# Turned context rows: written to memory once, loaded in cross attention

## The chip, the cores and the metric

The kernel runs on one core of one Trainium2 chip. The metric is the device time of one execution in microseconds. All data is fp32. One core has the engines TensorE (PE; its weight loads are shown apart as PEld), VectorE (DVE), ScalarE (ACT), GpSimd (POOL) and SyncE (SP, which only issues transfers here), and 16 DMA engines that serve the queues of all of them.

## What is computed

A two-layer Perceiver block: 16 batches of 64 latents x of width 256, and a context of 1601 rows of width 256 per batch.

```python
# layer 0
K = ctx @ Wk.T + bk ; V = ctx @ Wv.T + bv          # all 16 x 1601 rows
# each latent, head (16) and sample (5) reads two neighbouring rows of K and V at an
# offset that the query decides, weighs them, and attends over its 5 samples
x = x + sampled_attention(layer_norm(x), K, V)
x = x + self_attention(layer_norm(x))
x = x + moe_top2_of_8(layer_norm(x))
# layer 1: cross attention with 16 heads of 64
txt, img = ctx[:, :77], ctx[:, 77:]                # 77 and 1524 rows
q = heads(layer_norm(x) @ Wq)
out = softmax(q @ heads(txt @ Wk).T / 8) @ heads(txt @ Wv) \
    + softmax(q @ heads(img @ Wk_ip).T / 8) @ heads(img @ Wv_ip)
x = x + out @ Wo + bo
x = x + state_space(layer_norm(x))
x = x + moe_top4_of_32(layer_norm(x)) + shared_expert
```

The context thus enters twice: in layer 0 through the projection to K and V of every row, and in layer 1 through the image rows.

## The kernel before

P = 128 is the number of partitions, D = 256 the width, KC = 2 the number of 128-blocks in it, B = 16 the batches, M = 1601 the context rows.

**Order.** The instructions of TensorE, VectorE and ScalarE run in the order in which the program issues them (a manual schedule, from L1515 on). A scheduler places those of SP and GpSimd; a queue is served in its order, so a transfer on SP that waits holds up those behind it. A tile is taken from a pool by a tag with so many buffers (`bufs`); a new tile waits for the last user of the buffer it takes.

**Keys and values** (`keys_values`, L368 to L410). The rows of a batch go in spans (L236): three of 512 rows (128 partitions of r = RP = 4 neighbouring rows each) and a last one of 65 rows (r = 1). For each span

- `cx_load` (L239) loads the rows into `cx` on SP's queue, two spans ahead, two buffers;
- TensorE turns them in blocks of 128x128 (`transposes`, its matmul is L152; input to the matmul `ident`), ScalarE copies the turned blocks to `cxt` (L397, two buffers);
- one span later (`held`) `project` multiplies `cxt` with the weights `wkv` (L87, `st<-wkv,cxt`, 512 columns), ScalarE copies the result to `kv` (L381, two buffers), and one transfer on ScalarE's queue writes `kv` to the table of the batch in device memory (L384, `tab<-kv`): 16 heads x 512 bytes for each partition.

The main loop (L1529) takes one such step after the other and puts filler work between them: the sampling positions (`samples`), the text keys and values (`texts`, which writes `ktd`, L523), the first middle blocks (`middle`), and at given due times the gathers of the sampled rows from the tables by GpSimd (`g<-tab`, L428) and the sampled attention on VectorE.

**Cross attention** (class `Cross`, L896). For a batch, `loads` (L904) fetches the image rows as they are, `cn` (128 partitions of 11 rows, and 116 of one more; two buffers; a column of ones is added for the sum of the exponentials). `turn` (L926) transposes them once more, 24 blocks of 128x128 (L152, `mm<-ident,cn`), and VectorE and ScalarE copy the result to `cT` (one buffer). So the same image rows are turned by TensorE twice in the kernel, in keys and values and here. A `step` (L1059) then works on one pair of heads of the 8 in a batch: scores from the turned rows (`st<-qf,cT`, three groups of 512 columns), their maximum on VectorE (L1079), subtraction and exponential to `pt` (L1119, L1120, and L1122, L1123 for the last 116 rows), and in the next step the product of `pt` with `cn` (L1048). `qf` is the query folded with the key weights (`fold`, L1004). The last step of each batch calls the turn of the next one, between the output `out` (L1089) and the first product:

```python
if hp == NHP - 1:
    self.turn(b + 1)
if old:
    po = bank()[:, : D + 1]
    self.product(n - 1, 0, po)
```

The turn of batch 0 stands in `begin` (L1164), before the first step. Filler work of other parts (`side`, `mid`, `late`) is called from within the steps.

The order of the image rows is free: softmax and product sum over all of them, so any order will do as long as the scores and `cn` have the same.

Of the kernel before, what the change touches and what calls it, by code (L numbers as in the profile page):

```python
# [11 lines left out]
AF = mybir.ActivationFunctionType  # L12
ALU = mybir.AluOpType
# [4 lines left out]
P = 128  # L18
B, S, D = 16, 64, 256
M = 1601  # L20
KC = D // P
# [13 lines left out]
H1, HD1, INNER, TEXT = 16, 64, 1024, 77  # L35
IMG = M - TEXT
NHP = H1 // 2
CM = IMG // P
CR = IMG - CM * P
NCH = CM + 1  # L40
NB = NCH // 4


NST, NCONV = 16, 4
# [20 lines left out]
def perceiver_kernel(ctx: ExitStack, tc: tile.TileContext, a: dict, out: bass.AP):  # L65
    nc = tc.nc

    def mk(pool, shape, tag, dtype=F32, bufs=None):
        return pool.tile(list(shape), dtype, tag=tag, name=tag, bufs=bufs)
# [9 lines left out]
    def copy(i, o, x):  # L79
        if i % 2:  # L80
            nc.scalar.copy(o, x)  # L81
        else:
            nc.vector.tensor_copy(o, x)

    def mm(o, pairs):
        for i, (l, r) in enumerate(pairs):
            nc.tensor.matmul(o, lhsT=l, rhs=r, start=i == 0, stop=i == len(pairs) - 1)  # L87
# [59 lines left out]
    def transposes(blocks, ncol=P):  # L147

        rows = blocks[0].shape[0]
        t = bank().rearrange("p (i n) -> p i n", n=P)  # L150
        for i, b in enumerate(blocks):
            nc.tensor.transpose(t[:ncol, i, :rows], b, ident[:rows, :rows])  # L152
        return t

    def load(pool, tag, src, shape, bufs=None):
        t = mk(pool, shape, tag, bufs=bufs)
        nc.sync.dma_start(out=t, in_=src)
        return t
# [74 lines left out]
    sp = tpp  # L233


    spans = [(b, m0, RP if M - m0 >= RP * P else 1) for b in range(B) for m0 in range(0, M, RP * P)]  # L236
    cxs = {}

    def cx_load(i):  # L239
        if i < len(spans):  # L240
            b, m0, r = spans[i]
            w = min(P, M - m0)
            cx = cxs[i] = mk(kvp, [P, RP, D], "cx", bufs=2)
            nc.sync.dma_start(
                out=cx[:w, :r, :], in_=a["ctx"][b, m0 : m0 + w * r, :].rearrange("(p r) d -> p r d", r=r)
            )
# [121 lines left out]
    def keys_values():  # L368

        held = kv = None  # L370

        def project(i, cxt, q):
            nonlocal kv
            b, m0, r = spans[i]
            w = min(P, M - m0)
            if q == 0:
                kv = mk(kvp, [P, H0, RP, 2 * HD0], "kv", bufs=2)
            for c in range(2 * q, min(2 * q + 2, r)):
                pk = big()
                mm(pk[:w], [(cxt[:, c, k, :w], wkv[:, k, :]) for k in range(KC)])  # L380
                nc.scalar.copy(kv[:w, :, c, :], pk[:w].rearrange("p (h e) -> p h e", h=H0))  # L381
            if 2 * q + 2 >= r:
                tab = tables[b // 2].rearrange("n e -> (n e)").rearrange("(b h m e) -> b h m e", b=2, h=H0, e=2 * HD0)
                nc.scalar.dma_start(  # L384
                    out=tab[b % 2, :, m0 : m0 + w * r, :].rearrange("h (p r) e -> p h (r e)", r=r),
                    in_=kv[:w, :, :r, :].rearrange("p h r e -> p h (r e)"),
                )

        for i, (b, m0, r) in enumerate(spans):
            w = min(P, M - m0)  # L390
            cx = cxs.pop(i)
            cxt = mk(kvp, [P, RP, KC, P], "cxt")
            steps = (r + 1) // 2
            for q in range(steps):
                m = min(2, r - 2 * q)
                tp = transposes([cx[:w, 2 * q + t, k * P : (k + 1) * P] for t in range(m) for k in range(KC)])
                nc.scalar.copy(  # L397
                    cxt[:, 2 * q : 2 * q + m, :, :w].rearrange("p r k n -> p (r k) n"), tp[:, : KC * m, :w]
                )
                if q + 1 == steps:  # L400
                    cx_load(i + 2)
                if held:
                    for part in range((held[2] + 1) // 2):
                        if min(part, steps - 1) == q:
                            project(held[0], held[1], part)
                yield
            held = (i, cxt, r)
        for q in range((held[2] + 1) // 2):
            project(held[0], held[1], q)
        yield  # L410
# [485 lines left out]
    class Cross:  # L896
# [7 lines left out]
        def loads(self, b):  # L904
            if b >= B:
                return

            cn = self.cn[b] = mk(self.xc, [P, NCH, D + 1], "cn", bufs=2)
            nc.gpsimd.memset(cn[:, :, D:], 1.0)
            nc.sync.dma_start(  # L910
                out=cn[:, :CM, :D], in_=a["ctx"][b, TEXT : TEXT + CM * P, :].rearrange("(p c) d -> p c d", c=CM)
            )
            nc.sync.dma_start(out=cn[:CR, CM, :D], in_=a["ctx"][b, TEXT + CM * P :, :])

        def text_loads(self, b):
            if b >= B:
# [9 lines left out]
        def turn(self, b):  # L926

            if b >= B:
                return
            cn = self.cn[b]  # L930
            ct = self.ctx[b] = mk(self.xc, [P, KC, NCH * P], "cT", bufs=1)
            i = 0
            for k in range(KC):
                d = slice(k * P, (k + 1) * P)
                for c in range(0, CM, 4):
                    n = min(4, CM - c)
                    blocks = [cn[:, c + i_, d] for i_ in range(n)]
                    tp = transposes(blocks)
                    copy(i % 3, ct[:, k, c * P : (c + n) * P].rearrange("p (i n) -> p i n", n=P), tp[:, :n, :])
                    i += 1  # L940
                tp = transposes([cn[:CR, CM, d]])
                nc.scalar.copy(ct[:, k, CM * P : IMG], tp[:, 0, :CR])

                nc.scalar.copy(ct[:, k, IMG:], ct[:, k, : NCH * P - IMG])

        def queries(self, t, part):

# [94 lines left out]
        def product(self, n, part, po):  # L1042

            b = n // NHP
            pt, cn = pts[n % 2], self.cn[b]
            for c in range(part * 4, part * 4 + 4):
                w = P if c < CM else CR
                nc.tensor.matmul(po, lhsT=pt[:w, c, :], rhs=cn[:w, c, :], start=c == 0, stop=c == NCH - 1)  # L1048

        def turn_out(self, n):  # L1050
# [8 lines left out]
        def step(self, side=None, mid=None, more=None, late=None):  # L1059
# [11 lines left out]
            for i in range(NB):  # L1071
                if live:
                    s = big().rearrange("p (c n) -> p c n", n=P)
                    for c in range(4):
                        j = (i * 4 + c) * P
                        mm(s[:, c, :], [(ct[:, k, j : j + P], qf[:, k, :]) for k in range(KC)])
                    st.append(s)
                if live:
                    nc.vector.tensor_reduce(mp_[:, i, :], s.rearrange("p c n -> p n c"), AX.X, ALU.max)  # L1079
                    if i:  # L1080
                        nc.vector.tensor_tensor(mp_[:, 0, :], mp_[:, 0, :], mp_[:, i, :], ALU.max)
                if i == 1 and n - 2 < last:
                    self.turn_out(n - 2)
                if i == 1 and more is not None:
                    next(more, None)
                if i == 0:
                    tick(4.3)
# [25 lines left out]
            if live:  # L1113
                pt = pts[n % 2]
                for i in range(NB):
                    c0 = i * 4
                    m = 4 if i + 1 < NB else 3
                    o = pt[:, c0 : c0 + m, :]
                    nc.vector.tensor_tensor(o, st[i][:, :m, :], mc.to_broadcast([P, m, P]), ALU.subtract)  # L1119
                    nc.scalar.activation(o, o, AF.Exp)  # L1120
                o = pt[:CR, CM, :]
                nc.vector.tensor_tensor(o, st[-1][:CR, 3, :], mc[:CR, 0, :], ALU.subtract)  # L1122
                nc.scalar.activation(o, o, AF.Exp)  # L1123
            if late is not None:
                next(late, None)
            if old:
# [29 lines left out]
        def begin(self, xp):  # L1156
            self.xp = xp
            self.text_loads(0)
            self.weights(0, 0)
            yield  # L1160
            for part in range(3):
                self.queries(0, part)
                yield
            self.turn(0)  # L1164
            self.loads(1)
            yield
            self.text(0, 0)
            yield
            self.text(0, 1)
            self.text_turn(0, 0)  # L1170
            yield
            self.text_turn(0, 1)
            self.fold(0)
            yield
# [340 lines left out]
    with tc.manual_schedule(engines={ET.PE, ET.DVE, ET.Activation}):  # L1515
        for z in qbds:
            nc.gpsimd.memset(z, 0.0)
        for z in pts:
            nc.gpsimd.memset(z[:, CM, :], 0.0)
        nc.sync.dma_start(out=rsc, in_=a["rscale"].rearrange("(k p) -> p k", p=P))  # L1520
        nc.sync.dma_start(out=rws, in_=a["router0"].rearrange(kp, p=P))
        xbo = biases(const, "xbo", ("xbo",), a["bias_a"])["xbo"]
# [35 lines left out]
        xc = sx.enter_context(tc.tile_pool(name="xc", bufs=1))  # L1558
        cr = Cross(xc)
        cr.loads(0)  # L1560

        mids = middle(1, lp, single=True)
        while attended() < 12:
# [157 lines left out]
```

## Time and profile before

| | us |
|---|---|
| median of 3 runs | 3315.74 |
| lowest and highest | 3312.72, 3335.57 |
| the profiled execution | 3330.78 |
| its span | 3329.1 |
| PE busy in the span | 2961.7 (89%) |
| DVE busy | 1620.5 (49%) |
| ACT busy | 1024.3 (31%) |
| POOL busy | 809.0 (24%) |

The span is the time from the first to the last instruction of the profiled execution. Its mean granted TensorE clock was 0.944 of full speed. Keys and values end at about 715 us, cross attention runs from about 960 to 3040 us. A group of the profile is named by engine, line, operation and output<-input (partitions x elements); "mean ns of one" follows its busy time, and then the idle time of the engine before it, with what ended most of it. A matmul line gives first the tile of the stationary operand. The releasers are inferred from semaphores. In the table by stages each engine has its busy time and the number of its instructions; then come the granted clock, the mean busy share of the 16 DMA engines, and their rate.

### The profile page before, as it was taken

The numbers are of one execution on the slowest core, as the hardware profiler recorded it, in microseconds if no ns is written. First come the engines' busy times: TensorE is split into PE (matmuls) and PEld (weight loads), VectorE is DVE, ScalarE is ACT, GpSimd is POOL, SyncE is SP. The second block draws the span as 40 slices with busy tenths as digits, with TensorE's granted clock in tenths as the row PEclk, the third lists the DMA queues.
The fourth block names the chain that finished last, engine by engine and source line by source line (L and its number), as shares of the span: only waits on it lengthen the run. The fifth ranks groups of instructions, "written<-read, shape, count | busy, mean of one in ns | idle before, by whom it ended". The sixth has DMA issues, their size and how long they took to land.

```text
span 3329.1 us, 46406 instructions
## 1 busy us (share of the span) xinstructions
PE 2961.7 (89%) x17710; PEld 2420.5 (73%) x17710; DVE 1620.5 (49%) x4130; ACT 1024.3 (31%) x2366; POOL 809.0 (24%) x919
## 2 busy tenths in 40 slices
PE   8789887894878788889989999999999999998879
PEld 4444444562667777778878999999989999996666
DVE  3321113223334444445654335776577568665746
ACT  3233333322122221122333343333343344222421
POOL 0444434445334333432000001010001002000721
PEclk9889998996988899989999999999999999999999
DMA  7387755562321111111213542111112122003884
GB/s 230 100 152 160 219 162 155 169 183 55 116 65 24 43 42 55 26 54 41 73 38 116 165 128 72 56 60 50 49 61 55 50 70 65 30 1 119 254 235 121
DMA packets 338710, 326.19 MB, mean 98 GB/s; under 512 B 59301, under 2 KB 289097, under 8 KB 337977
## 3 DMA queue, kind: packets, MB, share of 16 engines
q1 hardware_dynamic: 186473, 226.04, 22.6%
q10 hardware_dynamic: 126640, 62.79, 6.8%
q0 software_dynamic: 25376, 34.39, 4.9%
q8 instruction: 141, 2.31, 0.3%
q14 instruction: 80, 0.66, 0.1%
HBM read 248.90 MB, written 74.22 MB: 97 GB/s over the span
## 4 chain that ended last, share of the span: by engine, by line
PE 74%; DVE 10%; another core or an unknown queue 5%; issue 5%; ACT 3%; DMA 2%; POOL 0%; SPq 0%; ACTq 0%; DVEq 0%; POOLq 0%
PE st L87 30%; PE mm L1048 19%; PE mm L87 16%; PE mm L152 4%; PE mm L1004 2%; DMA wg<-in_guT 1%; PE mm L1034 1%; PE mm L973 1%; DVE hs L1287 1%; DVE mp L1079 1%; PE mm L1098 1%; ACT pt L1120 1%; DMA w<-in_gate 0%; DVE pt L1119 0%
## 5 line engine op out<-in xcount | busy, mean ns | idle before, releaser
L428 POOL DMA_INDIRECT g<-tab,ig x640 | 610.3, 954 | 876.8 <-DVE ig L426 662.2
L87 PE MATMUL st<-qf,cT 128*128 128x128 f32 x6144 | 762.5, 282 | 57.0 <-ACT qf L1007 32.6
L87 PEld LDWEIGHTS st<-qf,cT 128*128 128x128 f32 x6144 | 740.3, 198 | 65.1 <-ACT qf L1007 36.4
L1048 PE MATMUL mm<-cn,pt 128*128 128x257 f32 (+1 forms) x3072 | 757.9, 391 | 0.2 <-ACT cT L81 0.2
L1048 PEld LDWEIGHTS mm<-cn,pt 128*128 128x128 f32 (+1 forms) x3072 | 565.7, 194 | 87.2 <-issue 2.0
L87 PE MATMUL st<-wkv,cxt 128*128 128x512 f32 (+1 forms) x832 | 400.8, 628 | 38.0 <-ACT kv L381 18.7
L1079 DVE TENSOR_REDUCE mp<-st 128x128 f32<-128x512 f32 x384 | 260.3, 687 | 249.7 <-PE st L87 203.6
L87 PEld LDWEIGHTS st<-wkv,cxt 128*128 128x128 f32 (+1 forms) x832 | 156.9, 198 | 210.9 <-issue 183.9
L1119 DVE TENSOR_TENSOR pt<-st,mc 128x512 f32<-128x512 f32 (+1 forms) x384 | 224.0, 638 | 169.7 <-ACT mc L1110 133.9
L1120 ACT ACTIVATE pt<-pt 128x512 f32<-128x512 f32 (+1 forms) x384 | 207.2, 588 | 53.3 <-DVE pt L1119 51.2
L381 ACT COPY kv<-st 128x512 f32<-128x512 f32 (+1 forms) x208 | 118.8, 593 | 217.7 <-PE st L87 118.7
L1110 ACT COPY mc<-mm 128x128 f32<-128x128 f32 x128 | 33.9, 265 | 412.2 <-PE mm L1108 324.5
L1100 DVE TENSOR_REDUCE xmx<-mm 128x1 f32<-128x128 f32 x128 | 37.3, 291 | 233.2 <-PE mm L1098 198.2
L1057 ACT COPY ot<-mm 128x256 f32<-128x256 f32 x128 | 47.5, 371 | 322.5 <-PE mm L152 290.2
L87 PE MATMUL mm<-xt,w 128*128 128x256 f32 x512 | 128.5, 405 | 16.5 <-issue 6.5
L87 PEld LDWEIGHTS mm<-xt,w 128*128 128x128 f32 x512 | 104.3, 205 | 43.6 <-issue 20.9
L460 DVE TENSOR_REDUCE smx<-sc 128x4 f32<-128x20 f32 x32 | 5.3, 166 | 242.2 <-ACT sc L458 230.4
L1293 POOL TENSOR_TENSOR ys<-ys,hc 128x512 f32<-128x512 f32 x64 | 81.5, 1273 | 160.6 <-DVE hc L1292 160.5
L1377 POOL DMA_INDIRECT xb<-xnd,row x55 | 55.7, 1012 | 244.5 <-PE mm L1034 199.8
L1024 ACT COPY yt<-mm 128x64 f32<-128x64 f32 x128 | 27.2, 212 | 269.2 <-PE mm L87 243.3
L397 ACT COPY cxt<-mm 128x512 f32<-128x512 f32 (+1 forms) x112 | 60.8, 544 | 111.6 <-PE mm L152 41.2
L87 PE MATMUL mm<-ot,wvi 128*64 128x64 f32 x1024 | 75.1, 227 | 21.3 <-ACT ot L1057 21.1
(442 smaller groups left out, 3916.5 us busy)
## 6 DMA issues: line engine op xcount, KB each, us to landing
tab<-kv ACTq DMA_DIRECT2D x48, 1024.0 KB
w<-in_gate SPq DMA_DIRECT2D x62, 512.0 KB
cx<-in_ctx SPq DMA_DIRECT2D x48, 512.0 KB
cn<-in_ctx SPq DMA_DIRECT2D x16, 1408.0 KB
wg<-in_guT SPq DMA_DIRECT2D x87, 256.0 KB
wk<-in_xwkiT SPq DMA_DIRECT2D x32, 512.0 KB
w<-in_lin SPq DMA_DIRECT2D x31, 512.0 KB
wd<-in_down1T SPq DMA_DIRECT2D x87, 128.0 KB
```

The source lines that it names most:

```text
L87: nc.tensor.matmul(o, lhsT=l, rhs=r, start=i == 0, stop=i == len(pairs) - 1)
L152: nc.tensor.transpose(t[:ncol, i, :rows], b, ident[:rows, :rows])
L381: nc.scalar.copy(kv[:w, :, c, :], pk[:w].rearrange("p (h e) -> p h e", h=H0))
L397: nc.scalar.copy(cxt[:, 2 * q : 2 * q + m, :, :w].rearrange("p r k n -> p (r k) n"), tp[:, : KC * m, :w])
L428: nc.gpsimd.indirect_dma_start(out=gf[:, (half * n + s) * 4 * HD0 : (half * n + s + 1) * 4 * HD0], out_offset=None, in_=tables[j], in_offs ...
L1004: nc.tensor.matmul(pf[:, k * P : (k + 1) * P], lhsT=w[:, hp % 4, k * P : (k + 1) * P], rhs=rhs, start=True, stop=True)
L1048: nc.tensor.matmul(po, lhsT=pt[:w, c, :], rhs=cn[:w, c, :], start=c == 0, stop=c == NCH - 1)
L1079: nc.vector.tensor_reduce(mp_[:, i, :], s.rearrange("p c n -> p n c"), AX.X, ALU.max)
L1119: nc.vector.tensor_tensor(o, st[i][:, :m, :], mc.to_broadcast([P, m, P]), ALU.subtract)
L1120: nc.scalar.activation(o, o, AF.Exp)
L1293: nc.gpsimd.tensor_tensor(y, y, hc, ALU.add)
L1377: nc.gpsimd.indirect_dma_start(out=x, out_offset=None, in_=xnd, in_offset=bass.IndirectOffsetOnAxis(ap=tb.row[:, i : i + 1], axis=0))
```

## The change

The turned image rows that the keys' and values' part has anyway are written to a tile `ctd` in device memory, 512 KB for a span, on SP's queue behind the load of a later span. The turn of cross attention becomes three loads from it, into three tiles `ct0` to `ct2` of one buffer each, and that of batch 0 is called right behind `cr.loads(0)`.

For this the spans of both parts must be the same: the 77 text rows come first as a span of their own (r = 1), then the image rows in spans of 512, 512 and 500 (128, 128 and 125 partitions of four rows). `cn` is loaded in the same three parts, so that its rows stand in the order of the turned ones. The missing three columns of the last span are filled with copies of others by a second, small copy on ScalarE, so that the whole 128x512 tile is written; their scores are computed but have no part in the product, which takes 125 partitions there. A softmax in a step is now three subtractions and three exponentials of 128x512 each, and the two memsets of `pts` go.

```diff
--- before.py
+++ after.py
@@ -35,10 +35,9 @@
 H1, HD1, INNER, TEXT = 16, 64, 1024, 77
 IMG = M - TEXT
 NHP = H1 // 2
-CM = IMG // P
-CR = IMG - CM * P
-NCH = CM + 1
-NB = NCH // 4
+SPAN = (P, P, 125)
+NB = len(SPAN)
+NCH = NB * RP
 
 
 NST, NCONV = 16, 4
@@ -233,13 +232,14 @@
     sp = tpp
 
 
-    spans = [(b, m0, RP if M - m0 >= RP * P else 1) for b in range(B) for m0 in range(0, M, RP * P)]
+    spans = [(b, m0, w, r) for b in range(B) for m0, w, r in [(0, TEXT, 1)] + [(TEXT + s * RP * P, w, RP) for s, w in enumerate(SPAN)]]
+    ctd = mk(dram, [B, NB, P, RP * KC * P], "ctd")
     cxs = {}
 
     def cx_load(i):
         if i < len(spans):
-            b, m0, r = spans[i]
-            w = min(P, M - m0)
+            b, m0, w, r = spans[i]
             cx = cxs[i] = mk(kvp, [P, RP, D], "cx", bufs=2)
             nc.sync.dma_start(
                 out=cx[:w, :r, :], in_=a["ctx"][b, m0 : m0 + w * r, :].rearrange("(p r) d -> p r d", r=r)
@@ -371,8 +371,7 @@
 
         def project(i, cxt, q):
             nonlocal kv
-            b, m0, r = spans[i]
-            w = min(P, M - m0)
+            b, m0, w, r = spans[i]
             if q == 0:
                 kv = mk(kvp, [P, H0, RP, 2 * HD0], "kv", bufs=2)
             for c in range(2 * q, min(2 * q + 2, r)):
@@ -386,8 +385,7 @@
                     in_=kv[:w, :, :r, :].rearrange("p h r e -> p h (r e)"),
                 )
 
-        for i, (b, m0, r) in enumerate(spans):
-            w = min(P, M - m0)
+        for i, (b, m0, w, r) in enumerate(spans):
             cx = cxs.pop(i)
             cxt = mk(kvp, [P, RP, KC, P], "cxt")
             steps = (r + 1) // 2
@@ -397,8 +395,15 @@
                 nc.scalar.copy(
                     cxt[:, 2 * q : 2 * q + m, :, :w].rearrange("p r k n -> p (r k) n"), tp[:, : KC * m, :w]
                 )
+                if r > 1 and w < P:
+                    nc.scalar.copy(
+                        cxt[:, 2 * q : 2 * q + m, :, w:].rearrange("p r k n -> p (r k) n"), tp[:, : KC * m, : P - w]
+                    )
                 if q + 1 == steps:
                     cx_load(i + 2)
+                    if r > 1:
+                        nc.sync.dma_start(out=ctd[b, (m0 - TEXT) // (RP * P)], in_=cxt.rearrange("p r k n -> p (r k n)"))
                 if held:
                     for part in range((held[2] + 1) // 2):
                         if min(part, steps - 1) == q:
@@ -907,10 +912,12 @@
 
             cn = self.cn[b] = mk(self.xc, [P, NCH, D + 1], "cn", bufs=2)
             nc.gpsimd.memset(cn[:, :, D:], 1.0)
-            nc.sync.dma_start(
-                out=cn[:, :CM, :D], in_=a["ctx"][b, TEXT : TEXT + CM * P, :].rearrange("(p c) d -> p c d", c=CM)
-            )
-            nc.sync.dma_start(out=cn[:CR, CM, :D], in_=a["ctx"][b, TEXT + CM * P :, :])
+            m0 = TEXT
+            for i, w in enumerate(SPAN):
+                nc.sync.dma_start(
+                    out=cn[:w, i * RP : (i + 1) * RP, :D], in_=a["ctx"][b, m0 : m0 + w * RP, :].rearrange("(p r) d -> p r d", r=RP)
+                )
+                m0 += w * RP
 
         def text_loads(self, b):
             if b >= B:
@@ -927,21 +934,9 @@
 
             if b >= B:
                 return
-            cn = self.cn[b]
-            ct = self.ctx[b] = mk(self.xc, [P, KC, NCH * P], "cT", bufs=1)
-            i = 0
-            for k in range(KC):
-                d = slice(k * P, (k + 1) * P)
-                for c in range(0, CM, 4):
-                    n = min(4, CM - c)
-                    blocks = [cn[:, c + i_, d] for i_ in range(n)]
-                    tp = transposes(blocks)
-                    copy(i % 3, ct[:, k, c * P : (c + n) * P].rearrange("p (i n) -> p i n", n=P), tp[:, :n, :])
-                    i += 1
-                tp = transposes([cn[:CR, CM, d]])
-                nc.scalar.copy(ct[:, k, CM * P : IMG], tp[:, 0, :CR])
-
-                nc.scalar.copy(ct[:, k, IMG:], ct[:, k, : NCH * P - IMG])
+            self.ctx[b] = [
+                load(self.xc, f"ct{i}", ctd[b, i].rearrange("p (r k n) -> p r k n", r=RP, k=KC), [P, RP, KC, P], 1) for i in range(NB)
+            ]
 
         def queries(self, t, part):
 
@@ -1044,7 +1039,7 @@
             b = n // NHP
             pt, cn = pts[n % 2], self.cn[b]
             for c in range(part * 4, part * 4 + 4):
-                w = P if c < CM else CR
+                w = SPAN[c // RP]
                 nc.tensor.matmul(po, lhsT=pt[:w, c, :], rhs=cn[:w, c, :], start=c == 0, stop=c == NCH - 1)
 
         def turn_out(self, n):
@@ -1072,8 +1067,7 @@
                 if live:
                     s = big().rearrange("p (c n) -> p c n", n=P)
                     for c in range(4):
-                        j = (i * 4 + c) * P
-                        mm(s[:, c, :], [(ct[:, k, j : j + P], qf[:, k, :]) for k in range(KC)])
+                        mm(s[:, c, :], [(ct[i][:, c, k, :], qf[:, k, :]) for k in range(KC)])
                     st.append(s)
                 if live:
                     nc.vector.tensor_reduce(mp_[:, i, :], s.rearrange("p c n -> p n c"), AX.X, ALU.max)
@@ -1113,14 +1107,9 @@
             if live:
                 pt = pts[n % 2]
                 for i in range(NB):
-                    c0 = i * 4
-                    m = 4 if i + 1 < NB else 3
-                    o = pt[:, c0 : c0 + m, :]
-                    nc.vector.tensor_tensor(o, st[i][:, :m, :], mc.to_broadcast([P, m, P]), ALU.subtract)
+                    o = pt[:, i * 4 : i * 4 + 4, :]
+                    nc.vector.tensor_tensor(o, st[i], mc.to_broadcast([P, 4, P]), ALU.subtract)
                     nc.scalar.activation(o, o, AF.Exp)
-                o = pt[:CR, CM, :]
-                nc.vector.tensor_tensor(o, st[-1][:CR, 3, :], mc[:CR, 0, :], ALU.subtract)
-                nc.scalar.activation(o, o, AF.Exp)
             if late is not None:
                 next(late, None)
             if old:
@@ -1161,7 +1150,6 @@
             for part in range(3):
                 self.queries(0, part)
                 yield
-            self.turn(0)
             self.loads(1)
             yield
             self.text(0, 0)
@@ -1515,8 +1503,6 @@
     with tc.manual_schedule(engines={ET.PE, ET.DVE, ET.Activation}):
         for z in qbds:
             nc.gpsimd.memset(z, 0.0)
-        for z in pts:
-            nc.gpsimd.memset(z[:, CM, :], 0.0)
         nc.sync.dma_start(out=rsc, in_=a["rscale"].rearrange("(k p) -> p k", p=P))
         nc.sync.dma_start(out=rws, in_=a["router0"].rearrange(kp, p=P))
         xbo = biases(const, "xbo", ("xbo",), a["bias_a"])["xbo"]
@@ -1558,6 +1544,7 @@
         xc = sx.enter_context(tc.tile_pool(name="xc", bufs=1))
         cr = Cross(xc)
         cr.loads(0)
+        cr.turn(0)
 
         mids = middle(1, lp, single=True)
         while attended() < 12:
```

## The prediction

> **What bounds the kernel now.** I read the chain of the last work first, then the slices of the span, then busy time by stage, and last the DMA queues of single transfers.
>
> ```profile
> PE   8789887894878788889989999999999999998879
> ...
> DMA  7387755562321111111213542111112122003884
> ```
> ```profile
> PE 74%; DVE 10%; another core or an unknown queue 5%; issue 5%; ACT 3%; DMA 2%; POOL 0%; SPq 0%; ACTq 0%; DVEq 0%; POOLq 0%
> PE st L87 30%; PE mm L1048 19%; PE mm L87 16%; PE mm L152 4%; PE mm L1004 2%; DMA wg<-in_guT 1%; PE mm L1034 1%; PE mm L973 1%; DVE hs L1287 1%; DVE mp L1079 1%; PE mm L1098 1%; ACT pt L1120 1%; DMA w<-in_gate 0%; DVE pt L1119 0%
> ```
>
> TensorE sets the time; L152, all transposes, is 4% of the span. The slices show where the DMA engines have room: little in the first quarter (keys and values), much after it. By stage:
>
> ```profile
> core 0: us, PE busy (x) PEld busy (x) DVE busy (x) ACT busy (x) POOL busy (x), PEclk, DMA share, GB/s
> 0.00:715.00 715.00, 608.15 (x1932) 331.36 (x1932) 183.29 (x604) 244.43 (x472) 294.98 (x319) 0.93 0.64 168
> 362.00:493.00 131.00, 112.85 (x326) 54.54 (x326) 20.05 (x63) 46.09 (x88) 51.29 (x54) 0.92 0.66 188
> ...
> 724.00:732.00 8.00, 7.42 (x35) 6.22 (x34) 1.80 (x5) 1.01 (x3) 0.83 (x1) 1.00 1.09 324
> ...
> 1990.00:3030.00 1040.00, 1033.85 (x7685) 948.35 (x7684) 675.86 (x1517) 366.24 (x890) 76.18 (x121) 1.00 0.17 50
> ```
>
> Keys and values (0:715) are TensorE-bound, but the 16 DMA engines are busy 64% of it. Cross attention (1990:3030) is TensorE without gaps, DMA at 17%. So the change takes TensorE work from a stage without DMA load and puts bytes on a stage that is already two thirds full.
>
> **Removed: the turns.** One turn on TensorE, between the last output matmul and the first product:
>
> ```profile
> 2903.98 0.45 PE L87 MATMUL mm<-ot,wvi 128*64 128x64 f32 x6
> 2904.36 2.96 PE L152 MATMUL mm<-ident,cn 128*128 128x128 f32 x24
> 2907.24 1.14 PE L1048 MATMUL mm<-cn,pt 128*128 128x257 f32 x4
> ```
>
> From 2903.98 + 0.23 to 2907.24 it takes 3.03 us, where other steps have 0.15: 2.88 us. Eleven of the 15 turns in the loop are like this, in steps with no idle TensorE: 11 x 2.88 = 31.7 us, all on the path. The first four (about 1100, 1250, 1397 and 1543 us) take 4.04, 4.04, 3.69 and 6.18, together 17.4 us over 0.15 each; there VectorE also waits about 10 us at a time for gathers, and I credit 14. The first turn (960 to 965) was in the start of cross attention; the query scaling on ScalarE is next late at 963, so 2 us. Sum -48. Its eight copies per turn on VectorE and ScalarE (585 to 618 ns the large ones) were beside it.
>
> In each step the softmax becomes three subtractions and three exponentials of 128x512 where there were four of each (the last two of 128x384 and 116x128). One instruction fewer on each engine, under 0.2 us per step, and TensorE is the limit in most: -2. Two gpsimd memsets at the start go: nothing, the first loads land later.
>
> **Added: three loads of 512 KB per turn**, into single buffers. A score group's buffer is read last at 2899.7, 2901.6 and 2903.7 in that step and needed again at 2910.8, 2912.7 and 2914.6: 11 us of cover each. The nearest row, a context load of the same size and 4 KB rows, is issued at 0.97 and lands at 3.92 us. Hidden by a factor of three, DMA share 0.17. But SP is in order: in two places of the new instruction order a load of another buffer that may still be in use stands between ct0 and ct2. Between 0 and 15; I take 3.
>
> **The keys' and values' part.** The matmul work is the same rows (1601 per batch); two small copies per batch on ScalarE (3 padded columns, about 0.25 us each), 34% busy there, are hidden by TensorE. What is new is on the queues: a write of 512 KB per image span on SP (1.5 MB x 16), behind the next context load, and transfers of 125 partitions. The nearest rows say how many engines a transfer uses: each ends with one 4-byte packet per engine. The table write of a 128-partition span and that of the 65-row tail, then the tail's load, then the two loads of cn (128 and 116 partitions):
>
> ```profile
> q10 hardware_dynamic: 2064, 1.05, 67.3%
> ```
> ```profile
> q10 hardware_dynamic: 1053, 0.13, 32.8%
> ```
> ```profile
> q1 hardware_dynamic: 78, 0.07, 11.6%
> ```
> ```profile
> q1 hardware_dynamic: 1544, 1.56, 48.5%
> ```
>
> 2064 = 2048 data + 16. 1053 = 65 rows x 16 heads + 13. 78 = 65 + 13. 1544 = 1408 + 16 and 116 + 4. So 128 partitions use 16 engines, 65 use 13 and 116 use 4: the largest divisor up to 16. This is the rule of the Trainium skill, "DMA: Bandwidth & Descriptors", section "Why a DMA increments its semaphore by 16 and not by 1": the largest number up to 16 that divides the slowest dimension takes part. No row has 125 partitions; the rule gives **5** (and 11 for the 77 text rows, no worse than 13).
>
> The row alone: the 128-partition table write moves data from 0.94 to 4.74 us after its issue, 128 packets of 512 B per engine, 28.9 ns each. If 125 partitions cost the same, nothing changes. By the rule, 2000 packets on 5 engines are 400 each: 400 x 28.9 = 11.6, landing at 12.5 us alone, and an estimated 13 to 20 when the same five engines carry gathers and loads too. The load of cx (25 rows of 4 KB per engine) and the third of cn (100 packets of 1 KB) take 5 to 6 us instead of 3.
>
> Who waits: kv has two buffers, so the first kv copy of a batch's first wide span waits for the write of the previous batch's last one. ScalarE is in order: behind that copy stand the next cxt copies, then TensorE runs out of score banks after about 11 us of matmuls. In the trace this wait is nearly nil:
>
> ```profile
>   DMA tab<-kv: 7.7, 3
> ```
>
> The cover from issue to the waiting copy is 6 to 16 us, in the batches without filler work (362:493, 33 us each) only 4 to 6. A write landing at 13 to 20 us there holds ScalarE 8 to 14 us, of which TensorE's banks hide about half: 7 us in each of the 4 such batches = 28. In the 12 batches with samples, text or the first middle blocks, 1.5 each = 18. In 217:250 loads already take over 9 us to land; there the write to ctd, for which the cxt buffer waits, adds 9. Sum **+55**. Ends: +10 (fillers cover all) and +120 (7.5 in all 16). A second look by load: on those five engines a batch gets 272 x 28.9 ns = 7.9 (table), 3.4 (cx: 17 rows at 0.2) and 4.8 (ctd: 24 rows) more: 28.5 becomes 44.7 us of 44.7, and 24 becomes 40 in a 33 us batch. They are full, which excludes a gain here and speaks for the middle of the range.
>
> **The stage at 716.** The row 724:732 is at a DMA share of 1.09: weights stream there and TensorE waits for them. 1.5 MB of ct come on top, at 324 GB/s 5 us; cn's third part goes over five engines; and all of these wait for the last table write, 8 us later than now. +14, between 5 and 25.
>
> **Sum** on the profiled run of 3330.78 us (span 3329.1): -48 - 2 + 55 + 14 + 3 = **+22**, 3353. The median shown, 3315.74, is 15 lower; the same +22 on it is **3338 us**, +0.7%. About 1% is what a measurement of this kernel tells from no change.
>
> **Rivals.**
> - *A, the forecast (0.45)*: gain of the turns eaten in the keys' and values' part by the five-engine write. 3338; own range 3305 to 3370.
> - *B, the load is hidden (0.20)*: as by the row alone: keys and values +5, stage at 716 +5: -40, **3276**. For it: 85% PE busy in 0:715, so there are gaps to shift into, and only the last span of each batch is thin. Against: kv waits for the whole write.
> - *C, ct comes late (0.10)*: the loads queue behind SP's waits and about 3 us at each of 15 boundaries take the place of the turns: -50 + 45 + 10 + 14 = +19, **3335**. For it: single buffers, in-order SP. Against: 11 us of cover.
> - *D, the five engines bound the first part (0.25)*: once a table write lands more than some 20 us after its issue (cover 6 to 16 plus the half that the banks hide), every batch stalls; at 7 us x 16 = 112 and 716's +14: **3395**. For it: the load sum of 44.7 of 44.7 above. It decides wherever the fillers' own transfers share those engines.
> - *That it doesn't do what it says*: the new instruction order on TensorE has no transpose of cn left, so excluded.
>
> **How the numbers follow.** Faster by over 1% (under 3283) comes from most of B: 0.17. Slower by over 1% (over 3349) is D, a third of A and a little of C: 0.43. The rest, 0.40, is A's body. 3270 to 3405 takes in B and D.
>
> **What would show it.** Right: no mm<-ident,cn; last steps of a batch 12.3 us long instead of 15.2; 1990:3030 shorter by about 29 us for its 10 turns; table writes of 2005 packets (2000 + 5) landing after 12 us or more; the wait of kv on tab<-kv growing from 7.7 us to over 50; the last st<-wkv at about 765 instead of 709. Wrong: 2016 packets (16 engines) or no growth of that wait (B), TensorE waiting for ct at L87 (C), or batches of 50 us and more throughout (D).

## The result, and the profile after

The changed kernel took 3365.29 us in the median of 4 runs (3361.46 to 3368.75) against 3325.65 for the kernel before (4 runs, 3312.72 to 3341.73): ratio **1.0122**, 95% interval 1.0093 to 1.0151. Slower, by 39.6 us in the medians where 22 was forecast; inside the range, 27 us above the forecast. The experiments further down ran later, on three chips on which the kernel before took 3053 to 3056 us (the record does not name the chip of this first pair); they are compared with runs and profiles from those chips only.

The slices of the span of the changed kernel:

```profile
PE   6686867788577888888989999999999999999879
...
DMA  7466666666332121221311563222122223103884
```

and the first lines of its chain of last work:

```profile
PE 68%; DVE 10%; another core or an unknown queue 6%; DMA 5%; issue 4%; ACT 4%; ACTq 3%; SPq 0%; POOL 0%; DVEq 0%; POOLq 0%
PE st L86 28%; PE mm L1043 19%; PE mm L86 14%; ACTq L383 3%; PE mm L151 3%; PE mm L999 2%; DMA wg<-in_guT 1%; DMA tab<-kv 1%; DMA cx<-in_ctx 1%; PE mm L1029 1%; ACT pt L1112 1%; DVE mp L1073 1%; DVE hs L1275 1%; PE mm L968 1%
```

A new member is in the chain: `ACTq L383`. It is no computation but the instruction on ScalarE that issues the table write. Its 3% of 3366 us is some 100 us, the size of what the first part has grown by. Two groups give the stages, by the first and last start in the view of one tile (durations min/median/max, then these two). Before, then after:

```profile
L87 PE MATMUL st<-wkv,cxt x832: 589/592/1222, 11.9 to 709.9; 128*128 128x512 f32 x154, 128*65 128x512 f32 x13
```
```profile
L86 PE MATMUL st<-wkv,cxt x832: 592/592/1221, 11.3 to 808.1; 128*128 128x512 f32 x103, 128*125 128x512 f32 x51, 128*77 128x512 f32 x13
L86 PE MATMUL st<-qf,ct x6144: 269/275/582, 1070.5 to 3050.1; 128*128 128x128 f32 x199
```

The scores before ran from 973.6 to 3011.7. So:

| stretch | before | after | change | forecast |
|---|---|---|---|---|
| to the last projection of keys and values | 709.9 | 808.1 | +98.2 | +55 |
| from there to the first score | 263.7 | 262.4 | -1.3 | +14 - 2 |
| first to last score | 2038.1 | 1979.6 | -58.5 | -46 - 2 + 3 |
| from there to the end of the span | 317.4 | 315.8 | -1.6 | 0 |
| span | 3329.1 | 3365.9 | +36.8 | +22 |

The windows of the two kernels with the same work in each row (last projection to first score; batches 0 to 5 of cross attention; batches 6 to 14). Before, then after:

```profile
710.40:973.60 263.20, 178.61 (x699) 139.45 (x697) 94.60 (x284) 55.76 (x112) 106.87 (x115) 0.80 0.36 103
973.60:1861.60 888.00, 764.33 (x5189) 687.00 (x5190) 435.40 (x1158) 229.53 (x565) 227.08 (x248) 0.93 0.18 53
1861.60:2913.90 1052.30, 1048.94 (x7812) 966.10 (x7811) 656.12 (x1453) 387.78 (x918) 82.92 (x129) 1.00 0.22 68
```
```profile
808.70:1070.50 261.80, 173.69 (x675) 135.40 (x673) 90.35 (x274) 54.25 (x106) 106.19 (x114) 0.80 0.39 110
1070.50:1926.20 855.70, 744.01 (x5045) 666.69 (x5046) 419.64 (x1086) 216.59 (x481) 226.66 (x248) 0.93 0.23 67
1926.20:2952.30 1026.10, 1022.90 (x7595) 942.63 (x7594) 630.97 (x1346) 370.77 (x793) 82.98 (x129) 1.00 0.27 83
```

Where TensorE has no gaps, nine batches are 26.2 us shorter, 2.91 each: within 0.03 us of the turn. The granted clock is the same in each pair of rows, and in the last pair the DMA share goes from 0.22 to 0.27 without harm. The end of a batch after the change:

```profile
2945.29 0.45 PE L86 MATMUL mm<-ot,wvi 128*64 128x64 f32 x6
2945.67 2.01 PE L1043 MATMUL mm<-cn,pt 128*128 128x257 f32 x8
```

The product follows the output at once. No wait of TensorE for the loads of ct shows anywhere in the loop.

Now the loss. The timeline of ScalarE in a batch with little filler work, after (start, duration, engine, line, operation, and in brackets the idle time before it with what ended it; `issue` is nothing that the profile shows, `remote` a releaser that it cannot name):

```profile
491.50 0.59 ACT L380 COPY kv<-st 125x512 f32<-125x512 f32 x1 [3.61 <-remote]
492.12 0.28 ACTq L383 DMA_DIRECT2D tab<-kv  x1
492.50 0.59 ACT L395 COPY cxt<-mm 128x512 f32<-128x512 f32 x1 [0.41 <-remote]
492.98 0.58 ACT L380 COPY kv<-st 77x512 f32<-77x512 f32 x1
493.59 11.62 ACTq L383 DMA_DIRECT2D tab<-kv  x1
505.26 1.07 ACT L395 COPY cxt<-mm 128x512 f32<-128x512 f32 x2 [11.70 <-issue]
508.89 1.07 ACT L380 COPY kv<-st 128x512 f32<-128x512 f32 x2 [2.56 <-DMA tab<-kv]
```

and the same place before the change:

```profile
444.04 0.37 ACTq L384 DMA_DIRECT2D tab<-kv  x1
444.45 0.58 ACT L397 COPY cxt<-mm 128x512 f32<-128x512 f32 x1 [0.44 <-issue]
445.58 0.58 ACT L381 COPY kv<-st 65x512 f32<-65x512 f32 x1 [0.55 <-issue]
446.19 0.39 ACTq L384 DMA_DIRECT2D tab<-kv  x1
446.63 0.58 ACT L397 COPY cxt<-mm 128x512 f32<-128x512 f32 x1 [0.46 <-ACT kv L381]
```

The issue of the 500-row write takes 0.28 us. The issue of the next one, for the 77 text rows, takes 11.62 us, and ScalarE stands in it: the copies to cxt and kv behind it wait, and with them TensorE. On TensorE in that place, and then its longest sum of waits in the first part, before and after (us in all, times, longest):

```profile
498.21 0.60 PE L151 MATMUL mm<-ident,cx 128*128 128x128 f32 x4
505.90 5.68 PE L86 MATMUL st<-wkv,cxt 128*128 128x512 f32 x8 [7.09 <-ACT cxt L395]
```
```profile
PE st L87 <- ACT kv L381: 18.7, 6, 8.0
```
```profile
PE st L86 <- ACT cxt L395: 51.0, 6, 14.8
```

Fifteen such issues take 3.4 to 18.6 us each; all 64 together last 164.0 us, before the change 24.3. The DMA queue of ScalarE in that stretch (491.9 to 512.1), packets, MB and share of 16 engines:

```profile
q10 hardware_dynamic: 3248, 1.18, 24.4%
```

3248 = 2000 + 5 and 77 x 16 + 11. The last 500-row write has the queue to itself (809.3 to 823):

```profile
q10 hardware_dynamic: 2005, 1.02, 26.7%
```

So the 500-row write does run on five engines and the text rows on eleven. In the trace the last data packet of each of the sixteen 500-row writes lands 13.0 to 25.3 us after its issue.

### The profile page after: what moved, and what is told of

It is laid out like the page before. It is cut to its first block, busy times and chain, and to the rows that moved or that the text cites. A ratio compares the mean times of both kernels' runs of the same rounds, so it can differ in the third digit from the quotient of the medians.

```text
span 3365.9 us, 45522 instructions
## 1 busy us (share of the span) xinstructions
PE 2920.2 (87%) x17326; PEld 2379.0 (71%) x17326; DVE 1577.0 (47%) x3938; ACT 993.9 (30%) x2174; POOL 807.9 (24%) x917
## 4 chain that ended last, share of the span: by engine, by line
PE 68%; DVE 10%; another core or an unknown queue 6%; DMA 5%; issue 4%; ACT 4%; ACTq 3%; SPq 0%; POOL 0%; DVEq 0%; POOLq 0%
PE st L86 28%; PE mm L1043 19%; PE mm L86 14%; ACTq L383 3%; PE mm L151 3%; PE mm L999 2%; DMA wg<-in_guT 1%; DMA tab<-kv 1%; DMA cx<-in_ctx 1%; PE mm L1029 1%; ACT pt L1112 1%; DVE mp L1073 1%; DVE hs L1275 1%; PE mm L968 1%
## 5 line engine op out<-in xcount | busy, mean ns | idle before, releaser
L86 PE MATMUL st<-qf,ct 128*128 128x128 f32 x6144 | 757.4, 281 | 41.6 <-issue 22.0
L86 PEld LDWEIGHTS st<-qf,ct 128*128 128x128 f32 x6144 | 734.5, 197 | 52.4 <-issue 26.8
L86 PE MATMUL st<-wkv,cxt 128*128 128x512 f32 (+2 forms) x832 | 405.2, 634 | 57.2 <-ACT cxt L395 51.0
L86 PEld LDWEIGHTS st<-wkv,cxt 128*128 128x128 f32 (+2 forms) x832 | 160.3, 202 | 231.9 <-issue 170.9
L1111 DVE TENSOR_TENSOR pt<-st,mc 128x512 f32<-128x512 f32 x384 | 241.2, 684 | 160.0 <-ACT mc L1104 126.7
L1112 ACT ACTIVATE pt<-pt 128x512 f32<-128x512 f32 x384 | 228.0, 629 | 52.6 <-DVE pt L1111 50.5
L380 ACT COPY kv<-st 128x512 f32<-128x512 f32 (+2 forms) x208 | 119.4, 592 | 242.3 <-PE st L86 120.3
L86 PE MATMUL mm<-xt,w 128*128 128x256 f32 x512 | 125.7, 400 | 24.0 <-DMA w<-in_gate 11.9
L151 PEld LDWEIGHTS mm<-ident,cx 128*128 128x128 f32 (+2 forms) x416 | 55.9, 153 | 58.1 <-issue 37.0
L828 DVE TENSOR_TENSOR act<-gl,mm 128x256 f32<-128x256 f32 x64 | 26.4, 418 | 147.7 <-ACT gl L827 102.1
```

Of the source, the lines that this page charges most:

```text
L1111: nc.vector.tensor_tensor(o, st[i], mc.to_broadcast([P, 4, P]), ALU.subtract)
```

## The experiments

**The theories.** I: the write on five engines holds ScalarE and is the whole loss of the first part (Ia: by the issue of the next write, Ib: by the kv buffer). II: the ctd writes, their bytes and the cxt buffers that wait for them. III: the new order of the spans. Results together; "last projection" and "scores" are from one profile of each, as in the table above. The expectations of the first four experiments (table write split, text write on SP, no ctd writes, spans only) were written before the two kernels had been run again, so their times are on the scale of the first pair; their ratios can be compared.

| kernel | ratio to before | interval | last projection | first to last score |
|---|---|---|---|---|
| before, again | 1.000 | 0.9989 to 1.0011 | 609.1 | 1900.0 |
| after, again | 1.0314 | 1.0294 to 1.0334 | 737.1 | 1850.9 |
| table write split | 0.9927 | 0.9911 to 0.9944 | 635.6 | 1850.2 |
| text write on SP | 1.0265 | 1.0248 to 1.0282 | 720.7 | 1853.6 |
| no ctd writes | 1.0271 | 1.0254 to 1.0288 | 731.8 | 1849.3 |
| spans only | 1.0418 | 1.0397 to 1.0440 | 732.1 | 1888.9 |
| all thin transfers split | 0.9892 | 0.9866 to 0.9919 | 626.9 | 1854.1 |
| text rows in the first wide span | 0.9854 | 0.9835 to 0.9873 | 615.8 | 1855.2 |
| own narrow kv | 1.0275 | 1.0247 to 1.0302 | 729.4 | 1853.7 |
| own narrow kv, and on SP | 1.0064 | 1.0043 to 1.0085 | 661.4 | 1848.9 |
| text rows in the first span, own narrow kv | 0.9825 | 0.9798 to 0.9852 | 612.6 | 1848.7 |

**The two kernels again**

> The changed kernel as it is, on the chip of the experiments (where the kernel before took 3056 us, not 3326), so that they have a profile beside them. If the stall of the thin write is the whole of the first part's loss and the ctd writes cost nothing, it stands with the one that leaves these writes out: ratio 1.02 to 1.03. If the ctd writes cost 20 us or more, above 1.035.

> The kernel before as it is, for the profile on this chip: ratio 1.00. With the other profiles it splits the differences by stage: if the theory of the thin write holds, its last st<-wkv stands near 630-640, as with the split table write, and first to last score near 1890, as with the spans alone.

On these chips the change costs more, 3.1%: +128.0 in the first part, -49.1 in the scores. The ratio was 1.0314, just above the 1.02 to 1.03 that I expected. The last st<-wkv of the kernel before stands at 609.1, lower than the 630 to 640 that I expected, so the split table write (next) does not undo quite all.

Not all of the 128.0 is time in which TensorE stands. The first part of the kernel before, of the changed one and of the one with the table write split (the columns are those of the windows above; the granted clock is the third number from the end):

```profile
0.00:609.10 609.10, 571.54 (x1916) 316.15 (x1917) 181.88 (x598) 245.31 (x468) 292.01 (x316) 0.98 0.74 196
0.00:737.10 737.10, 598.42 (x1915) 328.84 (x1916) 183.25 (x604) 245.31 (x500) 292.61 (x316) 0.91 0.69 196
0.00:635.60 635.60, 575.80 (x1915) 316.57 (x1916) 183.81 (x604) 243.73 (x500) 292.85 (x316) 0.97 0.83 227
```

For the same matmuls TensorE is busy 26.9 us longer in the changed kernel, at a granted clock of 0.91 where it was 0.98. With one transfer split both come back (575.8 us, 0.97), although that edit touches no matmul. In these runs the lower clock thus comes with the stalls; by what rule, they do not show. In the first pair it was 604.2 us at 0.93 and 615.5 at 0.89.

**The table write split**

```diff
-                nc.scalar.dma_start(out=tab[... m0 : m0 + w * r ...], in_=kv[:w ...])
+                for p0, p1 in (((0, 112), (112, 125)) if w == 125 else ((0, w),)):
+                    nc.scalar.dma_start(out=tab[... m0 + p0 * r : m0 + p1 * r ...], in_=kv[p0:p1 ...])
```

> The table write of the 125-partition span is split into 112 and 13 partitions (16 and 13 engines instead of 5); all else as in the changed kernel. Theory I (the thin table write holds ScalarE, in whose queue the next table write then takes up to 18.6 us to issue, 164 us over all 64): the issues fall back to 0.4 us each, the last st<-wkv from 808 to about 715-725, total about 3275-3285, ratio 0.985-0.99. Theory II (the bytes of the ctd writes and the cxt buffers that wait for them): little changes, 3350-3365. Theory III (the order of the spans, text first): little changes as well.

Ratio 0.9927, a swing of 3.9% for one transfer per batch: theory I, though short of the 0.985 to 0.99 that I expected of it. The first part is 101 us shorter than in the changed kernel (635.6 against 737.1). The same place on ScalarE:

```profile
407.79 0.59 ACT L380 COPY kv<-st 125x512 f32<-125x512 f32 x1 [1.13 <-PE st L86]
408.41 1.98 ACTq L384 DMA_DIRECT2D tab<-kv  x2
410.48 0.59 ACT L396 COPY cxt<-mm 128x512 f32<-128x512 f32 x1 [2.11 <-PE mm L151]
410.97 0.58 ACT L380 COPY kv<-st 77x512 f32<-77x512 f32 x1
411.58 0.56 ACTq L384 DMA_DIRECT2D tab<-kv  x1
```

Both halves are issued within 2 us, and the text write behind them in 0.56. The issues did not all fall back to 0.4 us: the 13-row piece mostly takes 1.6, and four times 3.3 to 7.8.

**The text write on SP's queue, and narrow kv tiles of its own**: two ways for ScalarE to be held, taken away singly and together, with the five-engine write in place throughout.

```diff
-                nc.scalar.dma_start(
+                (nc.scalar if r > 1 else nc.sync).dma_start(      # text write on SP
```
```diff
-                kv = mk(kvp, [P, H0, RP, 2 * HD0], "kv", bufs=2)
+                kv = mk(kvp, [P, H0, r, 2 * HD0], "kv" if r > 1 else "kvn", bufs=2)      # own narrow kv
```

> The 77-row table write is issued on SP's queue instead of ScalarE's; the 500-row write stays on five engines of ScalarE's queue. If it is the issue of the next write that is held behind the thin one (theory Ia), ScalarE is free and the first part gets 60-90 us shorter, total about 3275-3305 (SP may wait in its place and delay cx). If it is the kv buffer that the thin write frees too late (theory Ib, as the prediction had it), the first kv copy of the next wide span waits instead: gain under 30 us, total 3335-3365.

> The changed kernel, but the narrow span (77 rows) has kv tiles of its own, so that a wide span's kv waits for the wide span before the last one, not for the thin write just issued. The thin write stays on five engines, and the narrow write stays behind it on ScalarE's queue. If the issue of the narrow write is enough to hold ScalarE (some 10 us per batch), nothing changes: ratio 1.025-1.033. If the kv buffer was the wait that counts, as the prediction's step has it, 0.99-1.01.

> Both: own kv tiles for the narrow span, and its table write issued on SP's queue. Neither the issue nor a kv buffer then holds ScalarE behind the thin write, which still goes over five engines. If the loss is ScalarE being held, the first part comes back to 630-650 us, ratio 0.99-1.00. If the five engines are full (the prediction's sum of 40 to 45 us of load per batch, against 38 us that a batch takes on this chip), SP or cx waits take its place: 1.015 or more.

Either alone leaves the loss nearly where it was (1.0265 and 1.0275 of 1.0314). Why the first gives so little is in its waits (us in all, times, longest):

```profile
ACT kv L380 <- DMA tab<-kv: 182.2, 17, 17.3
```

In the changed kernel on these chips the same line has 41.2 us; what the issue had hidden, the kv buffer takes over, since both wait for the same thin write. With both gone the ratio falls to 1.0064 and the first part to 661.4. That is above the 0.99 to 1.00 that held ScalarE alone would give and below the 1.015 of full engines. Its waits show the rest:

```profile
ACT cxt L395 <- DMA ctd<-cxt: 47.5, 10, 12.3
PE mm L151 <- DMA cx<-in_ctx: 29.8, 11, 7.2
ACT kv L380 <- DMA tab<-kv: 29.3, 11, 9.7
```

The other transfers have shares on the five engines too; that these are full is argued from the waits, not shown by a run. Of 128 us in the first part, 75.7 go when the narrow write's issue and buffer no longer hold ScalarE (737.1 - 661.4); another 26 go only with the write spread over the engines (661.4 to 635.6). ScalarE is not quite free in this kernel: beside the waits above, three issues of wide table writes still take 4.2 to 6.4 us.

**No ctd writes**

```diff
-                    if r > 1:
-                        nc.sync.dma_start(out=ctd[b, ...], in_=cxt...)
-                load(self.xc, f"ct{i}", ctd[b, i]..., [P, RP, KC, P], 1)
+                load(self.xc, f"ct{i}", a["ctx"][b, min(TEXT + i * RP * P, M - RP * P) :][: RP * P]..., [P, RP, KC, P], 1)
```

> The 48 writes of ctd are left out, and ct is loaded from the untransposed context rows (same size and 4 KB rows), so the scores are of other data. Theory I: at most 15 us less, 3350-3365. Theory II (the bytes and the cxt buffers): most of the 98 us of the first part goes, total about 3275.

The writes are left out and ct is loaded from the rows as they are, in loads of the same size, so the scores are of other data. The first part is 5 us shorter (737.1 to 731.8). The ratio is 0.4% lower, but the spans of the two profiles differ by 2.5 us only (3142.8 and 3140.3). Theory II falls. Beside the thin write, 24 MB of writes cost almost nothing here.

**Spans only**

```diff
-                        nc.sync.dma_start(out=ctd[b, ...], in_=cxt...)
-            self.ctx[b] = [load(self.xc, f"ct{i}", ctd[b, i]..., [P, RP, KC, P], 1) for i in range(NB)]
+            for i, w in enumerate(SPAN):      # turned by TensorE from cn as before
+                for q in range(2):
+                    tp = transposes([cn[:w, i * RP + 2 * q + t, k * P : (k + 1) * P] for t in range(2) for k in range(KC)])
+                    copy(i * 2 + q, o[:, :, :w], tp[:, :, :w])
```

> Only the spans are changed (text first; 512, 512, 500 in both parts): no ctd, and cross attention turns cn by TensorE as before, 24 blocks per batch in the same place. Theory I: the first part is as slow as in the changed kernel (last st<-wkv 800-810), cross attention as before (2038 us from first to last score), total 3410-3425, ratio 1.025-1.03. Theory II: the first part as before, total about 3325.

The turn of batch 0 is back in `begin`, and the padding copies stand in the turn, not in keys and values. The worst of all, 1.0418 where I expected 1.025 to 1.03: the whole loss of the first part (732.1) without the gain of the turns (1888.9). As that loss is there without ctd and without the padding copies in keys and values, neither makes it. Between this and the changed kernel lie 1.0% or 32 us: what keeping the turned rows is worth once the spans are paid for.

**All thin transfers split**: `cx` and `cn` of the 125 partitions as well, in the same way.

> Beside the table write, also the loads of cx and of cn for the 125 partitions are split into 112 and 13. If only the table write matters, as with that alone split: 0.990 to 0.995. If the thin loads hold TensorE too (cx two spans ahead, cn a batch ahead: I doubt it), another 10-20 us less, 0.986-0.989.

0.9892 against 0.9927: in the middle of the two expectations, and the two intervals touch. The first part is 8.7 us shorter. Probably a small gain.

**Text rows in the first wide span**: no span of 125 partitions at all.

```diff
-SPAN = (P, P, 125)
+SPAN = (P, P, P)
+HEAD = M - RP * P * len(SPAN)                  # 65
-    ... [(0, TEXT, 1)] + [(TEXT + s * RP * P, w, RP) ...]
+    ... [(0, HEAD, 1)] + [(HEAD + s * RP * P, w, RP) ...]
-                if r > 1 and w < P:            # padding copies
-                    nc.scalar.copy(...)
+            nc.gpsimd.memset(cn[: (TEXT - HEAD) // RP, :RP, :], 0.0)
```

> A version without any span of 125 partitions: 65 text rows as the narrow span, then three spans of 512 whose first three partitions hold the other 12 text rows; in cross attention these rows' part of cn, with the column of ones, is set to zero by gpsimd after the load, so that they drop out of sum and product. No padding copies, table writes on 16, 16, 16 and 13 engines as before the change. If the loss of the first part is all from the 125 partitions, it is as long as in the kernel before and the turns' 35-40 us stay: ratio 0.985-0.988. If the ctd writes or the new order of the spans cost something, 0.99 or more.

> The version with 12 text rows in the first wide span (no 125 partitions), with own kv tiles for the narrow span as well. The kv copies there still wait 27 us for table writes in the first part. If these waits reach TensorE, 5-10 us less than without, 0.982-0.984; if TensorE's banks hide them, 0.985-0.986.

0.9854, first part 615.8: 6.7 us over the kernel before, which is what the new order of the spans and the ctd writes cost together, if anything (one profile of each, and the times of the kernel before scatter by 13 us); theory III falls with it. With own narrow kv tiles in addition, kv waits for table writes once (6.2 us, where it was 27.1), and the ratio is **0.9825**; as the intervals of the two overlap, the step between them is not shown. This is the better version of the change: faster than before by 1.5 to 2.0%, and all of its idea is in it.

## Why the prediction was right, and where its terms were off

**The sign and the cause** held. The 125 partitions run on five engines (2000 + 5 packets), as the rule of the Trainium skill that the prediction named ("DMA: Bandwidth & Descriptors") says. Alone, such a write was put at 12.5 us, and the last one, alone on its queue, lands after 13.0. The row alone (3276) would have been wrong; spread over 16 and 13 engines, the kernel is faster than before, as rival B had it for that case.

**"Who waits"** is the step that named the wrong instruction. It had the first kv copy of the next wide span wait for the buffer, with 6 to 16 us of cover. In the trace the narrow table write, a span earlier, waits first, in its issue, 1.5 to 6.7 us behind the thin one's; the wait of kv grew only from 7.7 to 34.9 us, not over 50. The run with the text write on SP shows that this mattered little: the copy waits 182.2 us then.

**The sum of +55 was short by 43.** The term of the batches without filler was about right: three that can be told apart (from 389.8 to 477.4 before, 446.7 to 560.9 after) grew by 26.6 us, 8.9 each against 7. The term of the other twelve, 1.5 each, was mis-sized: the remaining 72 us make some 5.5 each over 13. I had taken filler matmuls for cover, but these need ScalarE as well, to empty their banks, and it stood in the issue. TensorE's waits for copies of the text keys, one of the fillers, in the first part of the changed kernel:

```profile
PEld mm L86 <- ACT kts L525: 29.5, 4, 12.5
...
PE mm L86 <- ACT kts L525: 27.2, 4, 12.0
```

Before, they were 10.0 and 8.8 us in two. That is 18 of the 72; 11 us of the 98 are the longer busy time at the lower clock, for which the sum had no term. The 9 us for the ctd write at 217:250 were wrong the other way: the run without the writes gains 5 us in the whole first part. In effect rival D's stall, put at 7 us in every batch, came true at about 6 (98.2 over 16), if not evenly.

**The load sum** (44.7 of 44.7 us) was right in part only: with ScalarE freed of the narrow write, about 26 us of 128 remained for it. Its 24 us for a 33 us batch does not follow from the row shown: 0.66 of 33 is 22, which makes 38, not 40.

**The turns**: 2.91 us per batch measured where I had 2.88. In batches 0 to 5, I credited about 21 us (14, 2 x 2.88 and part of the 2 for the softmax) and they gave 32.3. The six turns removed there were 23.1 us long in all (17.4 and 2 x 2.88), so some 9 us are something else; the traces do not say what. In the later pair the same batches gave 22.8 (749.8 to 727.0). ct was hidden (3 forecast, nothing found). Rival C is out.

**The stage at 716**: +14 forecast, -1.3 measured. TensorE's waits for the gate weights grew, from 3.4 to 11.9 us, but the stretch as a whole did not; what gave way was not traced. In the later pair it grew by 5.6 (232.8 to 238.4).

**Luck.** This stage and the scores came out 13 us better each than I had set them, for reasons that the mechanism does not give, and made up for 27 of the 43. In the later pair, where the first part lost 128.0, the same change cost 3.1%; the range ends at 3405, 2.7% over the 3315.74 that it started from, so there it would have been too low.

## To carry over

When a tile's partition count changes, look at how many engines its transfers then use, in the 4-byte packets at their end, and split it (here 112 and 13) or shift its bounds (here to 128) so that the large part uses all 16. A slow transfer on the queue of a computing engine cost twice here: by its buffer, and by the engine that stands in the issue of the next one; taking one away showed next to nothing while the other waited for the same thing. Filler work is cover only if it needs no engine that is held.

## What was not expected of the hardware

An issue can hold its engine: 3.4 to 18.6 us for the write behind a five-engine write, where 0.28 to 0.4 is usual. In the later profile of the changed kernel it ended each time when some 330 to 560 of the thin write's 2000 packets had not landed, 66 to 112 per engine, although the thin write's own 400 per engine had been issued in 0.28 us. What limit this is, the runs do not say.

And the same kernel took 3326 us in the first runs and 3053 in the later ones. The nine batches of scores with no gaps in TensorE take the same in both profiles (1052.3 and 1052.4 us in the kernel before, both at a granted clock of 1.00). The difference is in the first part (709.9 and 609.1 us, of which TensorE is busy 604.2 and 571.5, at a clock of 0.93 and 0.98) and in the first four batches of scores (579.0 and 442.5 us, busy 477.2 and 430.6, at 0.91 and 0.99). So the larger share of it is waiting, and the rest goes with a lower clock; why the first runs waited more was not tried.
